# Layer 1's query tokens turned by VectorE with one-piece transfers and kept by squares, and the first batch's gathering in a written order

## The chip, the core and the metric

The kernel runs on one core of one Trainium2 chip. The time is device microseconds of one execution of the whole program; a value for a kernel is the median over several executions. One further execution is recorded by the hardware profiler, and every view quoted below comes from that execution. The engines are named as the profile names them: PE (TensorE matmuls), PEld (TensorE weight loads), DVE (VectorE), ACT (ScalarE), POOL (GpSimd) and SP (SyncE, which issues all DMAs here; its own queue is SPq).

## The reference, cut to what matters

Two batches of 1024 tokens with 256 features pass through two layers. All data are float32.

```python
x = x + L0_xattn(layernorm(x), ctx, ...)      # windowed cross attention, 8 heads
x = x + L0_ffn(layernorm(x), W1, b1, W2, b2)  # 8 groups of 256 tokens, linear
x = x + L1_xattn(layernorm(x), ctx, ...)      # 16 heads of 16, sigmoid scores:
    # q = query @ Wq.T * scale; scores = sigmoid(q k^T); o = (scores v) @ Wo.T
x = x + L1_ffn(layernorm(x), gamma_x, gamma_slot, slot_embeds, w1, w2)
    # xn, se = rms_norm(x), rms_norm(slot_embeds);  logits = xn @ se^T  (1024 slots)
    # slots = softmax_over_tokens(logits)^T @ xn
    # h = gelu(slots @ w1); processed = h @ w2
    # out = softmax_over_slots(logits) @ processed
```

## The kernel before, in words

The tokens are held as four blocks `xq[0..3]` of 512 tokens, each a tile of 128 partitions by 4 subtiles by 256 features; blocks 0 and 1 are batch 0, blocks 2 and 3 are batch 1. A matmul contracts over partitions, so a block that is to be multiplied from its feature side must first be turned: features onto partitions, tokens along the row.

The kernel has two ways to turn a block. `transposed` (line 120) lets PE multiply 128x128 pieces with an identity into a PSUM bank, eight of them for a block (line 125), and copies each of the two banks to SBUF with `nc.any.tensor_copy` (line 126), where the framework picks ACT or DVE. `turned` (line 128) lets DVE transpose 32x32 squares (four instructions at line 134, 128x256 each) into a tile `tr`, and then moves the squares across partitions with 16 DMAs from SP (line 143). In `turned` each DMA moves 32 partitions by 1 KB, but writes it in eight pieces of 128 B, since the destination row runs in token order.

The stages, in the order in which PE passes them: layer 0 (projections, `product`, `bias_rows`, `feed_forward`) up to about 103 us; layer 1's attention, a loop over the four blocks `q` and two halves `c` (`queries` at line 1120, scores at line 1187 with ACT's tanh at line 1196, `poT` at line 1221, `output` at line 1134), up to about 172 us; the logits of both batches (`logits`, line 223) up to 226 us; then for each batch the gathering of slots (`gather`, line 330), `hidden` (line 405), `processed` and `combined` (line 475).

Around the change: `layernorm` (line 704) computes the moments, writes the normalised block `hn` on DVE (line 708) and calls `transposed`. Layer 1's queries use it four times, `hTs[0]` before the loop and `hTs[q + 1]` inside it, on tiles `hn_a` and `hT_a`; layer 0's feed-forward uses it as `norm_ff` on `hn_f` and `hT_f`. The normalised slot rows are turned by `turn_slot_rows` into `seT` (through `tr_se`), and the tokens of the soft mixture by `turn_tokens` into `xhT` (through `tr_m`). `seT` is the moving operand of every logits matmul:

```python
    rhs=seT[:, n, dc, :],       # line 226, 512 elements in one run
    rhs=hTs[q][:, dc, :],       # line 1123, queries
```

The framework orders the instructions of each engine before the run: a planner simulates the program and takes the ready instruction that was emitted first. Each engine then runs its list strictly in that order. Three things bind the planner. `tc.keep_in_program_order` (the argument `late`) pins an instruction behind the one that was emitted just before it on its engine. Inside `tc.manual_schedule(engines=...)` the named engines keep the emission order among the instructions of the region, while where these fall among instructions from outside the region is still the planner's. A nested region orders only the engines that the enclosing one does not. From line 1237 on ACT is ordered this way.

In the last loop, `gather(b, c)` multiplies eight token tiles `lgs[b][s]` (`psl`), DVE writes the scaled slots `sl` (lines 338 and 340), `turn_slots` turns them (`pst`, line 349), and `turn` transposes parts of `ec` on DVE (line 275) and moves them with 16 DMAs from SP (line 284). `largest` and `spread` (lines 295 to 314) build the column maxima `mb` through `dg`; `less` (POOL, line 319) and `dispatch` (ACT, line 322) then prepare each `lgs[b][s]`.

Of the kernel before, what the change touches and what calls it, by code (L numbers as in the profile page):

```python
# [9 lines left out]
FP = mybir.dt.float32  # L10
# [5 lines left out]
P = 128  # L16
# [3 lines left out]
DC = D // P  # L20
NK = 64
QT = 4
QN = QT * P
NQ = B * S // QN
# [18 lines left out]
EC = NSLOT // P  # L43
ST = S // P
XW = D + 2
SQ = 32
R4 = P // SQ


@with_exitstack  # L50
def tile_kernel(
# [51 lines left out]
        ALU.add,  # L103
    )

    seT = const.tile([P, 2, DC, 512], FP, tag="seT", name="seT")

    def moments(xt, name):

# [7 lines left out]
        nc.gpsimd.tensor_tensor(rstd, rstd, m_half, ALU.pow)  # L117
        return mv, rstd

    def transposed(src, dst, name, side=0):  # L120

        for c in range(DC):
            pt = bank(f"pt_{name}_{c}", side)
            for t in range(QT):
                nc.tensor.transpose(pt[:, ts(t, P)], src[:, t, ts(c, P)], ident)  # L125
            nc.any.tensor_copy(dst[:, c, :], pt)

    def turned(src, dst, tr, late=False):

        for t in range(QT):
            turn = nc.vector.transpose(
                tr[:, :, :, t, :].rearrange("p r c n -> p c r n"),
                src[:, t, 0:D].rearrange("p (c r n) -> p c r n", c=DC, r=R4),
            )
            if late:
                tc.keep_in_program_order(turn)
        to = dst.rearrange("p c (t i n) -> p (c t) i n", t=QT, i=R4)  # L140
        for i in range(R4):
            for r in range(R4):
                nc.sync.dma_start(
                    out=to[ts(r, SQ), :, i, :],
                    in_=tr[ts(i, SQ), r].rearrange("p c t n -> p (c t) n"),
                )


    outr = out.rearrange("(q t p) d -> q p t d", t=QT, p=P)
# [61 lines left out]
    def logits(b, s):  # L211

        q, t = b * QB + s // QT, s % QT
        if s == 0:
            zcs[b] = stat.tile([P, ST], FP, tag="zc", name=f"zc_{b}")
            rmaxs[b] = pools["md"].tile([P, NSLOT], FP, tag="rmax", name=f"rmax_{b}")
        lg = keep[b].tile([P, NSLOT], FP, tag=f"lg_{s}", name=f"lg_{b}_{s}")
        lgs[b][s] = lg
        nm = stat.tile([P, 2], FP, tag="nm", name=f"nm_{b}_{s}")
        for n in range(NSLOT // 512):  # L220
            pl = bank(f"pl_{b}_{s}_{n}", 0)
            for dc in range(DC):
                nc.tensor.matmul(  # L223
                    pl,
                    lhsT=xhTs[q][:, dc, ts(t, P)],
                    rhs=seT[:, n, dc, :],
                    start=(dc == 0),
                    stop=(dc == DC - 1),
                )

            nc.vector.tensor_tensor_reduce(  # L231
                lg[:, ts(n, 512)], pl, zero.to_broadcast([P, 512]), -1.0,
                BIG if n == 0 else nm[:, 0:1], ALU.add, ALU.min, nm[:, n : n + 1],
            )

            rm = rmaxs[b][:, ts(n, 512)]
            if s == 1:
                nc.vector.scalar_tensor_tensor(
                    rm, lgs[b][0][:, ts(n, 512)], -1.0, pl, ALU.mult, ALU.max
                )  # L240
            elif s > 1:
                nc.vector.tensor_tensor(rm, rm, pl, ALU.max)
        if t == 0:

            ecs[q] = keep[b].tile([P, 2, QT, 512], FP, tag=f"ec_{q % QB}", name=f"ec_{q}")
        nc.scalar.activation(  # L246
            ecs[q][:, :, t, :],
            lg.rearrange("p (h n) -> p h n", h=2),
            AF.Exp,
            bias=nm[:, 1:2],  # L250
            scale=-1.0,
            accum_out=zcs[b][:, s : s + 1],
        )
# [35 lines left out]
    def largest(b):  # L289

        mT = stat.tile([P, EC], FP, tag="mT", name=f"mT_{b}")
        for h in range(EC // 4):
            pm = bank(f"pm_{b}_{h}", 1)
            for c in range(4):
                nc.tensor.transpose(pm[:, ts(c, P)], rmaxs[b][:, ts(4 * h + c, P)], ident)
            nc.vector.tensor_reduce(
                mT[:, ts(h, 4)], pm.rearrange("p (c n) -> p c n", c=4), AX.X, ALU.max
            )
        dg = pools["mw"].tile([P, EC, P], FP, tag="dg", name=f"dg_{b}")
        nc.vector.tensor_tensor(  # L300
            dg,
            ident.unsqueeze(1).to_broadcast([P, EC, P]),
            mT.unsqueeze(2).to_broadcast([P, EC, P]),
            ALU.mult,
        )
        mTs[b] = dg
# [11 lines left out]
    def less(b, s):  # L318
        nc.gpsimd.tensor_tensor(lgs[b][s], lgs[b][s], mbs[b], ALU.add)  # L319
# [368 lines left out]
    with (  # L688
# [12 lines left out]
        pes = fr[:, NCT : NCT + NPE].rearrange("p (c s) -> p c s", c=DC)  # L701
        b1s = fr[:, NCT + NPE :].rearrange("p (g c) -> p g c", g=NG)

        def layernorm(xt, name, side=0):
            mv, rstd = moments(xt, name)
            hn = lnp.tile([P, QT, D], FP, tag="hn", name=f"hn_{name}")
            for t in range(QT):
                nc.vector.tensor_scalar(  # L708
                    hn[:, t, :], xt[:, t, :], mv[:, t, 0:1], rstd[:, t : t + 1],
                    ALU.subtract, ALU.mult,  # L710
                )
            hT = lnp.tile([P, DC, QN], FP, tag="hT", name=f"hT_{name}")
            transposed(hn, hT, name, side)
            return hT

        wide = ExitStack()
# [62 lines left out]
        def bias(g):  # L779
            pb = bank(f"pbs_{g}", 1)  # L780
            nc.tensor.matmul(pb[:, 0:D], lhsT=ones, rhs=b2z[:, g, :], start=True, stop=True)
            bs = ffc.tile([P, D], FP, name=f"bs_{g}")
            nc.any.tensor_copy(bs, pb[:, 0:D])
            bss.append(bs)
# [2 lines left out]
        hTfs = {}  # L787

        def norm_ff(q, side=0):
            hTfs[q] = layernorm(xq[q], f"f0_{q}", side)  # L790

        def feed_forward(q, side=0):
            for i in range(QN // GN):
# [244 lines left out]
        with (  # L1038
# [21 lines left out]
            def turn_slot_rows(h):  # L1060

                for c in range(h * QT, (h + 1) * QT):
                    tc.keep_in_program_order(
                        nc.vector.scalar_tensor_tensor(
                            se[:, c, :], se[:, c, :], sn[:, c : c + 1], gg, ALU.mult, ALU.mult
                        )
                    )
                tr = lnp.tile([P, R4, DC, QT, SQ], FP, tag="tr", name=f"tr_se_{h}")
                turned(se[:, ts(h, QT), :], seT[:, h], tr, late=True)

# [39 lines left out]

            hTs, qTs, oTs = {}, {}, {}

            def queries(q):
                qTs[q] = a1.tile([P, C1, QN], FP, tag="qT", name=f"qT_{q}")
                for c in range(C1):
                    pq = bank(f"pq_{q}_{c}", 1)
                    for dc in range(DC):
                        nc.tensor.matmul(  # L1120
                            pq,
                            lhsT=wq1s[:, dc, ts(c, P)],
                            rhs=hTs[q][:, dc, :],
                            start=(dc == 0),
                            stop=(dc == DC - 1),
                        )
                    nc.any.tensor_copy(qTs[q][:, c, :], pq)
# [16 lines left out]
                    )  # L1144

            slot_norms()
            hTs[0] = layernorm(xq[0], "a1_0", 1)
            product(7)
            norm_ff(NQ - 1)
            turn_slot_rows(0)  # L1150
            bias_rows(7)


# [17 lines left out]
            )  # L1171
            queries(0)
            bias(7)
            work = ExitStack()
            for q in range(NQ):
                b = q * QN // S
                oTs[q] = a1.tile([P, C1, QN], FP, tag="oT", name=f"oT_{q}")
                for c in range(C1):
                    if c == 1 and q == 0:
                        turn_slot_rows(1)  # L1180
                    if c == 0 and q > 1:
                        norm_tokens(q - 2)
# [16 lines left out]
                    if c == 0:  # L1199
                        if q == 0:  # L1200
# [4 lines left out]
                            pools["mw"] = work.enter_context(  # L1205
                                tc.tile_pool(name="mw", bufs=1, reuse_waits="tile")
                            )
                        if q + 1 < NQ:
                            hTs[q + 1] = layernorm(xq[q + 1], f"a1_{q + 1}", 1)
                        if q > 0:  # L1210
                            output(q - 1, (0, 1) if q + 1 < NQ else (0,))
                        if 0 < q < 3:
# [21 lines left out]

    ctx.enter_context(tc.manual_schedule(engines={mybir.EngineType.Activation}))
    open_keep(1)
    open_pool("slp", side="right")
    for u in range(1, B * ST + 2):  # L1240
# [29 lines left out]
    nc.sync.dma_start(out=ms, in_=m12_in)  # L1270
    for b in range(B):
        slTs[b] = pools["slp"].tile([P, DC, NSLOT], FP, tag="slT", name=f"slT_{b}")
        for c in range(EC):
            gather(b, c)
            if c > 0:
                turn_slots(b, c - 1)
            if b == 0 and c in (1, 3, 5):
                turn(c // 4, c // 2 % 2, c == 5)
            if b == 1 and c % 2 == 0:
                turn(QB + c // 4, c // 2 % 2, True)  # L1280
            if b == 0:
                less(1, c)
                if c > 0:
                    dispatch(1, c - 1)
        if b == 0:
            dispatch(1, ST - 1)
            sum_weights()
        hidden(b)
        with tc.manual_schedule(engines={mybir.EngineType.DVE, mybir.EngineType.PE}):
            processed(b)  # L1290
            combined(b)

# [69 lines left out]
```

## Time and profile before

| what | value |
|---|---|
| median of 3 runs | 444.54 us (443.05 to 444.97) |
| the profiled execution's own time | 443.19 us |
| its span, first to last instruction | 441.4 us |
| PE busy | 430.4 us, 97% of the span |
| PEld busy | 319.1 us, 72% |
| DVE busy | 328.4 us, 74% |
| ACT busy | 114.7 us, 26% |
| POOL busy | 84.7 us, 19% |
| mean granted TensorE clock | 0.999 |

Busy time is a sum over an engine's instructions. The span leaves out 1.8 us of the profiled execution's own time. A matmul of float32 operands appears as two records, so `x16` stands for eight matmuls. The line numbers are those of the kernel before.

### The profile page before, as it was taken

What the parts mean: (1) busy time and instruction counts of PE and PEld (TensorE: products, weight loads), DVE (VectorE), ACT (ScalarE), POOL (GpSimd) and SP (SyncE); (2) the same over time, 40 slices, a digit from 0 to 9 for tenths busy, and PEclk for the clock granted to TensorE, in tenths of its full rate; (3) what the DMA queues carried; (4) which work ended last, traced back from release to release, by engine and by line L of the source; (5) the groups of instructions that cost most, each with busy time, mean ns of one, the idle gap of its engine ahead of it and who ended that gap; (6) DMA issues with size and microseconds to landing.
All of it is one profiled execution on the core that took longest, in us unless ns stands there. A gap on an engine that the chain in (4) does not pass through costs nothing.

```text
span 441.4 us, 6412 instructions
## 1 busy us (share of the span) xinstructions
PE 430.4 (97%) x2368; PEld 319.1 (72%) x2368; DVE 328.4 (74%) x735; ACT 114.7 (26%) x213; POOL 84.7 (19%) x84
## 2 busy tenths in 40 slices
PE   6999999999999999999999999999999999999996
PEld 5788898888645545444458864699998884499996
DVE  0587989899284787998787259995995568796956
ACT  1212334112345441343573405510000002530000
POOL 3012232234212111200887930000000000000000
PEclk9999999999999999999999999999999999999999
DMA  8996595400202132321043633332003666600002
GB/s 269 415 422 274 224 379 206 170 0 7 42 10 39 21 47 30 48 32 18 0 162 72 98 52 50 45 56 43 1 0 103 97 90 99 90 1 1 1 1 97
DMA packets 100641, 42.08 MB, mean 95 GB/s; under 512 B 94593, under 2 KB 96769, under 8 KB 99201
## 3 DMA queue, kind: packets, MB, share of 16 engines
q1 hardware_dynamic: 100610, 41.67, 35.4%
q8 instruction: 19, 0.31, 0.3%
q14 instruction: 12, 0.10, 0.1%
HBM read 28.03 MB, written 2.10 MB: 68 GB/s over the span
## 4 chain that ended last, share of the span: by engine, by line
PE 81%; DVE 15%; POOL 1%; ACT 1%; issue 1%; DMA 1%; ACTq 0%; POOLq 0%
PE psl L330 12%; PE pl L223 12%; PE pp L475 11%; PE pc L475 11%; PE pmh L405 11%; PE pmt L744 5%; DVE b2z L775 5%; PE pq L1120 3%; PE pf L1134 3%; PE psg L1187 2%; PE poT L1221 2%; PE po L802 2%; DVE hn_f L708 1%; DVE bn_f L113 1%; DVE bn_a L113 1%; PE pt_a L125 1%
## 5 line engine op out<-in xcount | busy, mean ns | idle before, releaser
L744 PE MATMUL pmt<-wg 128*128 128x256 f32 x256 | 58.9, 388 | 3.8 <-DMA wg<-in_wff_dram 3.8
L330 PE MATMUL psl<-xh,lg 128*128 128x258 f32 x256 | 58.7, 381 | 0.0
L744 PEld LDWEIGHTS pmt<-wg 128*128 128x128 f32 x256 | 49.2, 195 | 10.7 <-DMA wg<-in_wff_dram 4.1
L223 PE MATMUL pl<-seT,xhT 128*128 128x512 f32 x128 | 55.9, 593 | 0.0
L330 PEld LDWEIGHTS psl<-xh,lg 128*128 128x128 f32 x256 | 47.3, 190 | 7.1 <-issue 0.5
L223 PEld LDWEIGHTS pl<-seT,xhT 128*128 128x128 f32 x128 | 24.2, 190 | 29.1 <-issue 24.9
L319 POOL TENSOR_TENSOR lg<-lg,mb 128x1024 f32<-128x1024 f32 x16 | 37.2, 2361 | 30.8 <-DVE mb L172 30.8
L475 PEld LDWEIGHTS pp<-ms,mh 128*128 128x128 f32 x256 | 29.4, 192 | 1.0 <-issue 1.0
L475 PE MATMUL pp<-ms,mh 128*128 128x128 f32 x256 | 29.7, 276 | 0.0
L246 ACT ACTIVATE ec<-lg,nm 128x1024 f32<-128x1024 f32 x16 | 18.4, 1148 | 40.4 <-DVE nm L231 40.4
L775 DVE SCALAR_TENSOR_TENSOR b2z<-wg,fr,b2z 128x256 f32<-128x256 f32 x48 | 24.6, 516 | 0.5
L415 ACT ACTIVATE mh<-mh 128x512 f32<-128x512 f32 x32 | 19.2, 627 | 20.3 <-DVE mh L448 17.7
L405 PE MATMUL pmh<-slT,ms 128*128 128x512 f32 x48 | 24.0, 592 | 0.0
L475 PE MATMUL pc<-pr,ec 128*128 128x128 f32 x192 | 22.1, 275 | 0.0
L475 PE MATMUL pp<-m_sums,mh 128*128 128x128 f32 x192 | 22.1, 275 | 0.0
L338 DVE RECIPROCAL rz<-psl 128x1 f32<-128x1 f32 x16 | 2.5, 156 | 26.0 <-PE psl L330 26.0
L475 PEld LDWEIGHTS pc<-pr,ec 128*128 128x128 f32 x192 | 21.8, 192 | 0.0
L475 PEld LDWEIGHTS pp<-m_sums,mh 128*128 128x128 f32 x192 | 21.8, 192 | 0.0
L1196 ACT ACTIVATE sg<-psg 128x512 f32<-128x512 f32 x32 | 16.5, 603 | 17.0 <-PE psg L1187 17.0
L275 DVE STREAM_TRANSPOSE tr<-ec 128x512 f32<-128x512 f32 x32 | 20.1, 679 | 0.0
L322 ACT ACTIVATE lg<-lg 128x1024 f32<-128x1024 f32 x16 | 16.5, 1049 | 12.4 <-POOL lg L319 12.4
L486 DVE TENSOR_TENSOR mh<-mh,mh 128x1024 f32<-128x1024 f32 x16 | 18.5, 1219 | 1.5 <-PE pp L475 1.5
(187 smaller groups left out, 703.9 us busy)
## 6 DMA issues: line engine op xcount, KB each, us to landing
wg<-in_wff_dram SPq DMA_DIRECT2D x6, 2048.0 KB, 14.3
ec<-tr SPq DMA_DIRECT2D x128, 64.0 KB, 2.3
xT<-in_xT_dram SPq DMA_DIRECT2D x4, 512.0 KB, 12.8
x<-in_x_dram SPq DMA_DIRECT2D x4, 512.0 KB, 15.0
wg<-in_wff_dram SPq DMA_DIRECT2D x2, 1024.0 KB, 10.6
xhT<-tr_m SPq DMA_DIRECT2D x64, 32.0 KB, 2.0
ms<-in_m_dram SPq DMA_DIRECT2D x1, 2048.0 KB, 7.9
out_dram<-x SPq DMA_DIRECT2D x16, 128.0 KB, 1.8
```

Of the source, the lines that this page charges most:

```text
L223: nc.tensor.matmul(pl, lhsT=xhTs[q][:, dc, ts(t, P)], rhs=seT[:, n, dc, :], start=(dc == 0), stop=(dc == DC - 1),)
L246: nc.scalar.activation(ecs[q][:, :, t, :], lg.rearrange("p (h n) -> p h n", h=2), AF.Exp, bias=nm[:, 1:2], scale=-1.0, accum_out=zcs[b][:, ...
L275: ins = nc.vector.transpose(tr[:, :, :, t, :].rearrange("p r c n -> p c r n"), half[:, t, :].rearrange("p (c r n) -> p c r n", c=EC // 2, ...
L319: nc.gpsimd.tensor_tensor(lgs[b][s], lgs[b][s], mbs[b], ALU.add)
L322: nc.scalar.activation(lgs[b][s], lgs[b][s], AF.Exp, scale=-1.0)
L330: nc.tensor.matmul(pz[:, 0:XW], lhsT=lgs[b][s][:, ts(c, P)], rhs=xhs[b * QB + s // QT][:, s % QT, :], start=(s == 0), stop=(s == ST - 1),)
L405: nc.tensor.matmul(to, lhsT=lefts[i][:, ts(j, P)], rhs=slTs[b][:, i, 0:512] if i < 2 else rights[b][i], start=True, stop=True,)
L415: nc.scalar.activation(h, h, AF.Gelu)
L475: nc.tensor.matmul(to, lhsT=left(k, m), rhs=right[:, k, :], start=(k == 0), stop=(k == QT - 1),)
L486: nc.vector.tensor_tensor(dst, x, y, op)
L744: nc.tensor.matmul(pm[:, ts(hc, D)], lhsT=w1g[:, oc, ts(hc, P)], rhs=w2g[:, oc, :], start=(oc == 0 and hc == 0), stop=(oc == OC - 1 and hc ...
L775: nc.vector.scalar_tensor_tensor(acc, weights[g][1][:, oc, :], b1s[:, g, oc : oc + 1], acc, ALU.mult, ALU.add)
```

## The change

1. Layer 1's query blocks no longer pass through PE. `norm_queries(q)` normalises the block as before (`normed`) and calls `turned_by_square`: DVE's four transposes into `tr_a`, then 16 DMAs into `hTs[q]`, whose layout is now by squares, so that each DMA writes 1 KB per partition in one piece. Three `hTs` buffers are kept. Blocks 0, 1 and 2 are emitted before the loop, block 3 in its first round.
2. `seT` is laid out in the same way and filled with `turned_by_square`.
3. The two matmul groups that read them take the tokens through `in_order`, a view of 16 runs of 32 elements.
4. `turn_slot_rows(0)` is emitted later, after `bias(7)`, and `turn_slot_rows(1)` one round later.
5. `norm_ff` copies PSUM to SBUF on ACT for blocks 2 and 3; before, the framework chose.
6. The first batch's gathering loop is a region in which DVE and PE keep the emission order. Its three `turn` calls come after steps 0, 1 and 4 instead of 1, 3 and 5, and the last of them is no longer pinned.
7. `dg` moves from its own buffer to the buffer of `mb` (batch 0) or `rmax` (batch 1).

```diff
+IN_ORDER = {mybir.EngineType.DVE, mybir.EngineType.PE}
+ACT_ORDER = {mybir.EngineType.Activation}
...
-    seT = const.tile([P, 2, DC, 512], FP, tag="seT", name="seT")
+    seT = const.tile([P, 2, R4, DC, QT, SQ], FP, tag="seT", name="seT")
...
-    def transposed(src, dst, name, side=0):
+    def transposed(src, dst, name, side=0, out=nc.any.tensor_copy):
...
-            nc.any.tensor_copy(dst[:, c, :], pt)
+            out(dst[:, c, :], pt)
...
+    def turned_by_square(src, dst, tr, late=False):
+
+        squares(src, tr, late)          # the four DVE transposes, as in turned()
+        for i in range(R4):
+            for r in range(R4):
+                nc.sync.dma_start(
+                    out=dst[ts(r, SQ), i].rearrange("p c t n -> p (c t n)"),
+                    in_=tr[ts(i, SQ), r].rearrange("p c t n -> p (c t n)"),
+                )
+
+    def in_order(x, dc):
+
+        return x[:, :, dc].rearrange("p i t n -> p t i n")
...
-                    rhs=seT[:, n, dc, :],
+                    rhs=in_order(seT[:, n], dc),
...
-        dg = pools["mw"].tile([P, EC, P], FP, tag="dg", name=f"dg_{b}")
+        dg = pools["md"].tile([P, EC, P], FP, tag=("mb", "rmax")[b], name=f"dg_{b}")
...
         def norm_ff(q, side=0):
-            hTfs[q] = layernorm(xq[q], f"f0_{q}", side)
+            out = nc.any.tensor_copy if q < QB else nc.scalar.copy
+            hTfs[q] = layernorm(xq[q], f"f0_{q}", side, out)
...
-                turned(se[:, ts(h, QT), :], seT[:, h], tr, late=True)
+                turned_by_square(se[:, ts(h, QT), :], seT[:, h], tr, late=True)
...
+            def norm_queries(q, late=False):
+
+                hn = normed(xq[q], f"a1_{q}")
+                hTs[q] = a1.tile([P, R4, DC, QT, SQ], FP, tag="hTa", name=f"hTa_{q}", bufs=3)
+                tr = lnp.tile([P, R4, DC, QT, SQ], FP, tag="tr", name=f"tr_a_{q}")
+                turned_by_square(hn, hTs[q], tr, late)
...
-                            rhs=hTs[q][:, dc, :],
+                            rhs=in_order(hTs[q], dc),
...
             slot_norms()
-            hTs[0] = layernorm(xq[0], "a1_0", 1)
+            norm_queries(0)
             product(7)
             norm_ff(NQ - 1)
-            turn_slot_rows(0)
+            norm_queries(1)
+            norm_queries(2)
             bias_rows(7)
...
             queries(0)
             bias(7)
+            turn_slot_rows(0)
             work = ExitStack()
             for q in range(NQ):
...
                 for c in range(C1):
                     if c == 1 and q == 0:
+                        norm_queries(3, True)
+                    if c == 1 and q == 1:
                         turn_slot_rows(1)
...
-                        if q + 1 < NQ:
-                            hTs[q + 1] = layernorm(xq[q + 1], f"a1_{q + 1}", 1)
...
-        for c in range(EC):
-            gather(b, c)
-            if c > 0:
-                turn_slots(b, c - 1)
-            if b == 0 and c in (1, 3, 5):
-                turn(c // 4, c // 2 % 2, c == 5)
+        with tc.manual_schedule(engines=(IN_ORDER, ACT_ORDER)[b]):
+            for c in range(EC):
+                gather(b, c)
+                if c > 0:
+                    turn_slots(b, c - 1)
+                if b == 0 and c in (0, 1, 4):
+                    turn(c // 4, c % 2)
...
```

More of the change, by code (lines that the diff above doesn't have):

```diff
@@ L125, in transposed, with squares @@
                 nc.tensor.transpose(pt[:, ts(t, P)], src[:, t, ts(c, P)], ident)
-            nc.any.tensor_copy(dst[:, c, :], pt)
-    def turned(src, dst, tr, late=False):
+            out(dst[:, c, :], pt)
+    def squares(src, tr, late=False):
         for t in range(QT):
@@ L139, in turned @@
                 tc.keep_in_program_order(turn)
+    def turned(src, dst, tr):
+        squares(src, tr)
         to = dst.rearrange("p c (t i n) -> p (c t) i n", t=QT, i=R4)
@@ L702, in tile_kernel, with normed @@
         b1s = fr[:, NCT + NPE :].rearrange("p (g c) -> p g c", g=NG)
-        def layernorm(xt, name, side=0):
+        def normed(xt, name):
             mv, rstd = moments(xt, name)
@@ L711, in layernorm @@
                 )
+            return hn
+        def layernorm(xt, name, side=0, out=nc.any.tensor_copy):
+            hn = normed(xt, name)
             hT = lnp.tile([P, DC, QN], FP, tag="hT", name=f"hT_{name}")
-            transposed(hn, hT, name, side)
+            transposed(hn, hT, name, side, out)
             return hT
@@ L1231, in tile_kernel @@
             output(NQ - 1)
-    ctx.enter_context(tc.manual_schedule(engines={mybir.EngineType.Activation}))
+    ctx.enter_context(tc.manual_schedule(engines=ACT_ORDER))
     open_keep(1)
@@ L1272, in tile_kernel @@
         slTs[b] = pools["slp"].tile([P, DC, NSLOT], FP, tag="slT", name=f"slT_{b}")
-        for c in range(EC):
-            gather(b, c)
-            if c > 0:
-                turn_slots(b, c - 1)
-            if b == 0 and c in (1, 3, 5):
-                turn(c // 4, c // 2 % 2, c == 5)
[L1279 to L1282, printed above, removed]
-                if c > 0:
-                    dispatch(1, c - 1)
+        with tc.manual_schedule(engines=(IN_ORDER, ACT_ORDER)[b]):
+            for c in range(EC):
+                gather(b, c)
+                if c > 0:
+                    turn_slots(b, c - 1)
+                if b == 0 and c in (0, 1, 4):
+                    turn(c // 4, c % 2)
+                if b == 1 and c % 2 == 0:
+                    turn(QB + c // 4, c // 2 % 2, True)
+                if b == 0:
+                    less(1, c)
+                    if c > 0:
+                        dispatch(1, c - 1)
         if b == 0:
@@ L1288, in tile_kernel @@
         hidden(b)
-        with tc.manual_schedule(engines={mybir.EngineType.DVE, mybir.EngineType.PE}):
+        with tc.manual_schedule(engines=IN_ORDER):
             processed(b)
```

## The prediction

> **What bounds the kernel now.** I read first the table by stretches of the span, then who waited on PE, then the chain that ended last in order of time, and last the DMA issues and DVE's and SP's own instructions around the change.
>
> The table by stretches has for each engine its busy time and record count; the first figure after the stretch is its length.
>
> ```profile
> 99.00:165.00 66.00, 65.65 (x335) 39.42 (x336) 45.29 (x125) 26.94 (x54) 13.18 (x18) 1.00 0.18 27
> 165.00:226.00 61.00, 60.93 (x163) 28.05 (x162) 50.70 (x134) 22.88 (x35) 19.14 (x15) 1.00 0.16 24
> 226.00:233.00 7.00, 6.33 (x28) 4.21 (x27) 4.94 (x7) 5.62 (x7) 4.00 (x2) 1.00 0.83 303
> 233.00:259.00 26.00, 26.00 (x128) 22.48 (x127) 12.09 (x30) 8.46 (x8) 23.63 (x12) 1.00 0.52 78
> ```
>
> The reader is to see PE without a hole in all four (65.65 of 66.00 us, 26.00 of 26.00) at a granted clock of 1.00, and DVE with room in the first (45.29 of 66.00). A microsecond of PE work taken out here ends the program a microsecond earlier, as long as nothing new makes PE wait. The waits on PE, in whole:
>
> ```profile
> PE pmt L744 <- DMA wg<-in_wff_dram: 3.8, 1, 3.8
> ...
> PE pb L314 <- DVE dg L300: 0.7, 1, 0.7
> ...
> PE po L802 <- DVE hT_f L126: 0.4, 1, 0.4
> ```
>
> The 3.8 us stands at the start of the program. The 0.4 us is one that the change touches: a feed-forward of layer 0 waits for the second half of a turned block, copied by DVE. The chain in order of time (start, length) shows the four turnings that are to go:
>
> ```profile
> 105.69 0.87 PE pt_a L125 x8
> ...
> 123.83 0.87 PE pt_a L125 x8
> ...
> 131.40 1.07 PE psg L1187 x8
> 132.47 1.02 PE pt_a L125 x8
> 133.49 3.46 PE pf L1134 x16
> ...
> 144.71 1.02 PE pt_a L125 x8
> ...
> 155.88 1.07 PE psg L1187 x8
> 156.95 1.93 PE pf L1134 x8
> ```
>
> All four lie on the chain, between PE work on both sides.
>
> **What goes: 3.5 us of PE.** Four blocks of eight transposes, one record each. Where PE changes from `psg` to another form some 0.15 us is added to whatever follows: `pt_a` takes 1.02 after `psg` and 0.87 elsewhere, and `pf` x8 takes 1.93 after `psg` where half of 3.46 is 1.73. That addition passes to `pf`, so I count 4 x 0.87 = 3.48. PE starts a transpose every 0.109 us (0.87/8), while its record lasts 273 ns; the records overlap. The Trainium skill (TensorE: Matmul & The Clock Gate, Part 4: PE-mode transpose) gives about 275 ns for one in a kernel and says that the full clock does not engage for it. By that figure 32 of them would be an estimated 8.8 us; the trace has the record's length alike, but starts 0.109 us apart at clock 1.00, so the row decides.
>
> The eight PSUM copies into `hT_a` go too (five on ACT at 0.59 us, three on DVE at 0.67 us). Nobody but `pq` waited for them.
>
> **Feed-forward copies on ACT: 0.4 us.** `pt_f` of block 2 ends at 97.85 us; ACT copied the first half from 97.62 to 98.21, DVE the second from 98.62 to 99.30, and PE stood 0.40 us. With both on ACT the second ends about 98.80, just as PE has finished what it has (its last record before the wait starts at about 98.5 and ends at 98.95). Gain 0.4, at worst 0.
>
> **What comes on DVE: hidden.** Per block four transposes, 128x256, at 0.335 us a start (four in 1.42 us for `tr_se`): 5.7 us in all, less 2.0 of copies. Block 0 falls before 99 us, where DVE is busy 36.3 of 39.0 us, but it is ahead: the bias sums of group 7 end at 96.4 us and PE uses them at 118.5. The other three fall between 102 and 131 us, where the slot rows' 1.4 us at 106 move away. If the cover fails, one block's 1.4 us would show.
>
> **What comes on SP, and whether the blocks land in time.** 64 DMAs are added to SP's one queue, and 32 (`seT`) change shape. No row has 32 partitions by one piece of 1 KB. From above: the eight-piece transfers, 609 ns each on SP and 2.0 us to land. From below: the loads of one piece per partition, 328 ns. The output stores, 128 partitions by one 1 KB piece, are the nearest in shape: 337 at least, 400 in the median. I take 0.40, so a block is 6.4 us of SP and lands 2 us later.
>
> ```profile
> 107.66 32.28 SPq L143 DMA_DIRECT2D seT<-tr_se  x32
> 148.53 52.76 SPq L143 DMA_DIRECT2D xhT<-tr_m  x64
> ```
>
> SP is idle before 107.66 since its last weight load at 75.7 us, which is no longer queued behind anything of this change if block 0 is normalised where it is now (83.3 to 84.6 us). I follow each block. Block 0: transposes by 86, landed by 95; queries at 115. Block 1: its input is final at 97.0, normalising at about 102.5, transposes by 105, landed by 114; queries at 126.7 less 1.7 saved by then, so 125.0. Block 2: input at 106.2, its `hn` buffer free after `pt_f` at 113.5, transposes by 116, landed 125; needed at about 136. Slot rows 0: behind `vsum` (115.2), transposes by 119, landed 131. Block 3: input at about 123.7, transposes at 130, landed 139; needed at 148. Slot rows 1: behind `oT` of block 1 (about 136), landed 148; needed by the first logits. `xhT` of block 0, still in eight pieces: transposes at 148.4 less 3.2, so 145.2; 16 x 0.61 and 2.0 bring it to 157.0. The first logits matmul (162.97 before) wants it at 159.5. All in time, with 2.5 us left where 2.6 were before. A `tr` buffer is reused every second block; each earlier user has landed by then.
>
> Two new waits on DVE have something behind them: slot rows 1 and block 3 sit between `oT` instructions that `pf` wants at once, with no `pt_a` in between to cover. The pair at 155.88 and 156.95 shows `pf` following `psg` directly without a hole, `oT` being done meanwhile. I take 0 and keep 1 us as the upper end.
>
> **Strided reads by PE: 0.** 80 matmuls (160 records of 0.43 us, 68 us together) read 16 runs of 32 elements. The nearest row is `pk` at line 1077, whose moving operand is two runs of 64: 0.89 us for eight records, 111 ns each, against 112 ns for contiguous 128-column products (25.10 us for 224, line 475). One break costs nothing that 0.01 us in eight records can show; at that grain (1.3 ns) 15 breaks in 160 records could be 3 us. Below nothing is excluded, since a contiguous read is already at PE's pace. I take 0, keep 3.
>
> **The written order: 0.4 us lost.** At 226 to 233 us PE fills the wait for `dg` with 16 records of `psl`.
>
> ```profile
> 226.16 1.47 PE L330 MATMUL psl<-xh,lg 128*128 128x258 f32 x6
> 227.47 0.60 PE L295 MATMUL pm<-ident,rmax 128*128 128x128 f32 x4
> 227.90 2.56 PE L330 MATMUL psl<-xh,lg 128*128 128x258 f32 x10
> 231.14 1.98 PE L314 MATMUL pb<-dg,ones 128*128 128x512 f32 x4 [0.67 <-DVE dg L300]
> ```
>
> ACT prepares `lgs[0][4..7]` only from 227.80 to 231.68, 0.97 us each, so these 16 cannot be step 0 alone; some belong to step 1. In emission order step 1 must follow step 0's last: 14 records fit before `pb`, and two (2 x 0.22) come later. The region leaves `pb`'s place to the planner, so the fill itself stays; were it lost whole, it costs 16 x 0.22 = 3.5. Behind 233 us PE is full either way, and the order of `psl` and `pst` is the same. `turn` after step 4 waits about 1 us on DVE for its buffer's DMAs (issued 236 to 247, landed 249); `sl` of step 5 is queued behind it and is ready at 253, needed at 255. `dg` in other buffers: `mb`'s copies must wait for all of `pb`, which DVE's copy, the last one, did anyway: 0.
>
> **Sum.** -3.5 - 0.4 + 0.4 = -3.5 us. The profiled execution took 443.2 us (span 441.4 and 1.8 around it): 439.7. It lies at the low end of the three runs (443.05 to 444.97); their middle is 444.0, so I add 0.8 and forecast 440.5 as a median, 0.9% under 444.54.
>
> A rule speaks against the change: the Trainium skill (VectorE: DVE Perf Modes, Rules for kernel authors) would turn 128x128 on TensorE where PSUM will do. By path length the rows agree with it: 0.87 and two copies of 0.6 are 2.1 us, the new way 1.4 + 6.4 + 2.0 = 9.8. Were that on the path, four blocks would cost 4 x 7.7 = 31 us more; by the times above none is.
>
> **Rivals.** *SP's queue becomes the bound (slower).* If one-piece transfers take SP as long as the eight-piece ones, the queue never empties from block 2 on: 116 + 64 x 0.61 + 9.8 + 2.0 = 166.8 us for the first `xhT`, wanted at 159.5. PE stands 7.3 us there: 439.7 + 7.3 + 0.8 = 447.8. It decides from 0.50 us an issue on (116 + 64x + 11.8 = 159.5). For it: 609 ns in 96 such rows; against: 328 to 400 in every one-piece row. *The gain is eaten (no change).* The planner orders anew from simulated landing times; a fill of the kind at 226 us lost whole (3.5) or an `oT` or a block late by 2 to 3 us leaves 442.5 to 444.5. For it: PE's strict order and 64 more DMAs it must guess; against: the margins above, mostly over 8 us. *Strided reads cost (slower).* From 5% on the 68 us they eat the whole gain; at 10%, 447.3. Against: `pk`.
>
> **Chances.** Forecast 0.64 (its own range 438.5 to 442.0), SP's queue 0.12, gain eaten 0.18, strided reads 0.06. The range for 8 in 10 runs from 438.5 to 445.0: it takes in the forecast and the eaten gain and leaves out the two slower ones. About 0.5% (2.2 us) can be told from no change here: faster 0.66 (the forecast and the best of the eaten gains), within 0.5% 0.17, slower 0.17.
>
> **What would show it.** Right: no `pt_a` in the chain, `pq` and `pl` still at 0.43 us a start, DMAs into `hTa` and `seT` at about 0.4 us on SP, PE's stretch from 99 us to the first logits 3.9 us shorter, `pb` about 3.5 us earlier. Wrong: a wait of `pq` or `pl` on `tr_a`, `tr_se` or `tr_m`; `pf` waiting for `oT`; a longer hole at `dg`; a later last weight load on SP.

## The result, and the profile after

The changed kernel took 455.63 us in the median of six executions (455.17 to 457.22), the kernel before 444.36 in the median of six (443.05 to 444.97) on the same chip: a ratio of 1.026, with a 95% interval of 1.024 to 1.028. The forecast was 440.5 us. The profiled execution took 455.48 us, with a span of 453.7 us.

The table by stretches, for the first two of the four shown of before (length; then busy us and records of PE, PEld, DVE, ACT and POOL; granted clock; DMA share; GB/s):

```profile
99.00:165.00 66.00, 61.85 (x298) 35.58 (x296) 47.35 (x134) 24.70 (x50) 14.25 (x18) 0.97 0.20 45
165.00:226.00 61.00, 52.87 (x137) 24.78 (x138) 41.80 (x115) 15.20 (x24) 7.05 (x10) 0.92 0.22 33
```

Before, PE stood 0.35 us in the first and 0.07 in the second; now it stands 4.15 and 8.13, and the granted clock, 1.00 before, is 0.97 and 0.92. (The other two stretches now hold other work, since all from 180 us on runs 12 us later.) The waits on PE say whom it stood for:

```profile
PE pl L243 <- DMA xhT<-tr_m: 9.5, 1, 9.5
...
PE pf L1166 <- DVE oT L1262: 2.7, 1, 2.7
...
PE psl L350 <- ACT lg L342: 0.6, 2, 0.4
PE pb L334 <- DVE dg L320: 0.6, 1, 0.6
```

Two of these are new and large: 9.5 us before the first logits, for a transfer, and 2.7 us before a `pf`, for DVE. The 0.4 us for `hT_f` is gone. SP's own instructions show where both come from (start, length; 48 issues in one line are three blocks):

```profile
90.13 39.66 SPq L159 DMA_DIRECT2D hTa<-tr_a  x48
129.90 10.03 SPq L159 DMA_DIRECT2D seT<-tr_se  x16
140.04 10.02 SPq L159 DMA_DIRECT2D hTa<-tr_a  x16
150.16 10.90 SPq L159 DMA_DIRECT2D seT<-tr_se  x16
161.18 53.18 SPq L149 DMA_DIRECT2D xhT<-tr_m  x64
```

Sixteen one-piece transfers take SP 10.0 us, 0.63 from start to start; the median record is 589 ns, where the eight-piece ones have 609. From 108.1 to 171.7 us, where the first block's `xhT` is out, SP has no pause over 0.44 us. The first `xhT`, whose squares DVE had finished by 149.7, is issued at 161.18 and landed at 173.0. The chain that ended last shows both holes:

```profile
127.93 3.10 DMA hTa<-tr_a
...
131.16 1.42 DVE tr_a L133 x4
132.58 0.65 DVE oT L1262
133.27 4.96 PE pf L1166 x14
...
171.04 1.95 DMA xhT<-tr_m
...
173.13 5.91 PE pl L243 x8
```

In the first four lines DVE cannot turn block 3, since its `tr` buffer still holds block 2, whose last transfer lands at 131.0; `oT` stands behind that on DVE, and PE behind `oT`. In the last two the transfer ends PE's long wait. Besides, `pf` x14 takes 4.96 us (3.29 at the full clock) and `pl` x8 5.91 (3.60 before): the granted clock was 0.73 from 134 to 139 us and 0.67 from 173 to 180.

Just ahead of the first `xhT` the chain lists a `tr_m` at 159.82 us. By DVE's own records that is block 1's; block 0's had been there since 149.7. The chain names the releaser that came last by the records; what the issue waited for was its turn in the queue.

The place where PE fills the wait for `dg`, now (the timeline of PE, from the second `psl` group on):

```profile
240.03 0.60 PE L350 MATMUL psl<-xh,lg 128*128 128x258 f32 x2
241.02 0.70 PE L350 MATMUL psl<-xh,lg 128*128 128x258 f32 x2 [0.39 <-ACT lg L342]
241.97 0.70 PE L350 MATMUL psl<-xh,lg 128*128 128x258 f32 x2 [0.24 <-ACT lg L342]
243.24 1.98 PE L334 MATMUL pb<-dg,ones 128*128 128x512 f32 x4 [0.57 <-DVE dg L320]
```

In the written order PE waits for `lg` twice and puts 12 records ahead of `pb` where 16 were (the prediction had counted on 14). From the last group but one of `pm` to the first `pst` it is 11.61 us (237.82 to 249.43), 10.76 before.

### The profile page after: what moved, and what is told of

It is laid out like the page before. It is cut to its first block, busy times and chain, and to the rows that moved or that the text cites. A ratio compares the mean times of both kernels' runs of the same rounds, so it can differ in the third digit from the quotient of the medians.

```text
span 453.7 us, 6450 instructions
## 1 busy us (share of the span) xinstructions
PE 430.9 (95%) x2336; PEld 317.6 (70%) x2336; DVE 330.6 (73%) x746; ACT 113.0 (25%) x210; POOL 85.3 (19%) x84
## 4 chain that ended last, share of the span: by engine, by line
PE 72%; DVE 16%; SPq 6%; DMA 2%; issue 2%; ACT 1%; POOL 1%; ACTq 0%; DVEq 0%; POOLq 0%
PE pl L243 13%; PE psl L350 12%; PE pp L495 11%; PE pc L495 11%; PE pmh L425 11%; DVE b2z L799 4%; SPq L159 4%; PE pmt L768 3%; PE pf L1166 3%; SPq L149 2%; DVE hn_f L728 2%; PE pq L1152 2%; PE poT L1255 1%; DVE bn_f L115 1%; DVE bn_a L115 1%
## 5 line engine op out<-in xcount | busy, mean ns | idle before, releaser
L243 PE MATMUL pl<-seT,xhT 128*128 128x512 f32 x128 | 58.2, 613 | 9.5 <-DMA xhT<-tr_m 9.5
L768 PEld LDWEIGHTS pmt<-wg 128*128 128x128 f32 x256 | 49.2, 194 | 10.7 <-DMA wg<-in_wff_dram 3.9
L251 DVE CUSTOM_DVE_ANT_0 lg<-pl,zero 128x512 f32<-128x512 f32 x16 | 10.9, 678 | 14.4 <-PE pl L243 14.4
L1166 PE MATMUL pf<-w1s,oT 128*128 128x256 f32 x64 | 17.3, 420 | 2.7 <-DVE oT L1262 2.7
```

Source lines behind the costliest of these rows:

```text
L243: nc.tensor.matmul(pl, lhsT=xhTs[q][:, dc, ts(t, P)], rhs=in_order(seT[:, n], dc), start=(dc == 0), stop=(dc == DC - 1),)
L768: nc.tensor.matmul(pm[:, ts(hc, D)], lhsT=w1g[:, oc, ts(hc, P)], rhs=w2g[:, oc, :], start=(oc == 0 and hc == 0), stop=(oc == OC - 1 and hc ...
L1166: nc.tensor.matmul(pf[:, ts(k, D)], lhsT=oTs[q][:, c, ts(2 * i + k, P)], rhs=wo1s[:, c, :], start=(c == 0), stop=(c == C1 - 1),)
```

## The experiments

Four theories. **S:** SP needs some 0.63 us for an issue whatever its pieces, and 96 issues ahead of the first `xhT` make it late. **B:** the two `tr` buffers make DVE wait, and `oT` behind it. **R:** PE is slowed by reading 16 runs of 32. **W:** the written order costs 0.85 us. "Before" is the kernel before, run on the same chip in the same series: 443.3 us in the first two series, 443.6 and 444.2 in the others.

**four_issues: the same bytes in a quarter of the issues.**

```diff
-        for i in range(R4):
-            for r in range(R4):
-                nc.sync.dma_start(out=dst[ts(r, SQ), i]..., in_=tr[ts(i, SQ), r]...)
+        for i in range(R4):
+            nc.sync.dma_start(out=dst[ts(i, SQ)]..., in_=tr[ts(i, SQ)]...)
```

> Each block and each half of the slot rows moves in 4 DMAs of 32 partitions x 4 KB in place of 16 of 32 partitions x 1 KB: the same bytes, a quarter of the issues (the squares stay in their group of partitions, so the values read differ; PE's work is the same). Theory S (SP's queue: about 0.63 us an issue whatever its pieces, 96 of them ahead of the first xhT): 72 issues fewer take 45 us off the queue, xhT is issued as soon as tr_m is turned (about 146) and lands near 157, both holes (9.5 and 2.7 us) and the low clock behind them go: 439 to 442. Theory R (PE is slowed by what it reads, 16 runs of 32): nothing changes in PE's reads, so 455. If an issue's time goes with its bytes (4 KB: 4 times as long), SP is as full as before: 455. Theory W (the written order alone) 455.

Measured: 439.78 us, 0.992 of before (0.990 to 0.994). SP's instructions:

```profile
139.47 2.42 SPq L158 DMA_DIRECT2D seT<-tr_se  x4
145.79 52.50 SPq L149 DMA_DIRECT2D xhT<-tr_m  x64
```

This kernel leaves out the crossing of partitions, so its output is another one. An issue of 4 KB a partition holds SP as long as one of 1 KB did (0.59 us in the median), the first `xhT` goes out at 145.79, as the forecast had it (145.2), and neither hole is left; the clock is 1.00 from 8.5 us to the end of PE's work. Everything else of the change is still in it, the strided reads and the written order among them. So S holds, R falls, and W is small. The longest row of `pl` says the same of R, before and in the changed kernel:

```profile
210.21 15.61 PE L223 MATMUL pl<-seT,xhT 128*128 128x512 f32 x36
222.33 15.61 PE L243 MATMUL pl<-seT,xhT 128*128 128x512 f32 x36
```

The time is close to the forecast's (440.5), but with SP held 2.4 us for a block, and not the 6.4 that the forecast had.

**tr_three: a third `tr` buffer.**

```diff
-  tag="tr"                    # tr_se, tr_a
+  tag="tr", bufs=3
...
-  tag="xhT", bufs=3
+  tag="xhT", bufs=2           # for the space
```

> The changed kernel with three tr buffers in place of two (one xhT buffer less, for the space). Theory B (DVE stands on a tr buffer, oT is queued behind it): the two DVE waits of 3.3 us go, and the hole of 2.7 us before pf at 133 with them and the low clock behind it (1.9): 455.6 - 4.6 = 451. Theory S (the sum of the issues on SP): the hole at 133 goes too, but xhT of block 0 still lands at 173, since SP's queue is full from 108 on, so PE stands longer before pl (9.5 + 4.6 = 14 us): 455 to 456.

Measured: 455.44 us, 1.027 (1.025 to 1.030). Waits on PE:

```profile
PE pl L243 <- DMA xhT<-tr_m: 8.7, 1, 8.7
...
PE pq L1152 <- DMA hTa<-tr_a: 3.6, 1, 3.6
```

DVE's waits on `tr` and the hole before `pf` are gone, and the time stays. SP issues the first `xhT` at 161.75 (161.18 in the changed kernel). The hole did not all go to `pl`, as I had said: 3.6 us stand before `pq`, because block 3's transfers now come too late for a PE that is 3.9 us ahead (`psg` at 146.72 for 150.57). B is a symptom of S here.

**pe_queries: the query blocks back on PE, all else as changed.**

```diff
-            norm_queries(0)
+            hTs[0] = layernorm(xq[0], "a1_0", 1)      # and so for blocks 1 to 3, as before
...
-                            rhs=in_order(hTs[q], dc),
+                            rhs=hTs[q][:, dc, :],
```

> The changed kernel with the query blocks turned on PE as before (64 issues fewer on SP, 32 transposes back on PE); the slot rows stay in squares and are read so, the feed-forward copies stay on ACT, the gathering stays in its written order. S: the loss goes with the queue: 444.4 - 0.4 (copies on ACT) + 0.85 (written order) = 444.8. R: pl still reads seT in runs of 32, 96 of its 160 strided records remain: 447 or more. If the loss were the written order's: 454.

Measured: 448.51 us, 1.011 (1.008 to 1.014): none of the three. The hole is still there, smaller (2.7 us for `xhT` and a `pl` x8 of 5.37 us). SP's instructions tell why:

```profile
118.88 33.94 SPq L159 DMA_DIRECT2D seT<-tr_se  x32
152.94 53.30 SPq L149 DMA_DIRECT2D xhT<-tr_m  x64
```

Before, the 32 issues for `seT` began at 107.66 and the first `xhT` at 148.53; here they begin at 118.88, because the change emits the slot rows later, and `xhT` goes out 4.4 us later with no query transfer in the queue at all (its squares were ready at 149.06, 0.6 us later than before; the rest is the queue). My expectation had counted what the queue holds and not where the slot rows stand in it. Hole 2.7, clock 1.8, written order 0.9 and 0.4 gained make 5.0; 5.2 were measured.

**two_blocks: the kernel before with blocks 0 and 1 by VectorE.**

```diff
+            NDVE = 2
...
-                        if q + 1 < NQ:
+                        if NDVE <= q + 1 < NQ:
                             hTs[q + 1] = layernorm(xq[q + 1], f"a1_{q + 1}", 1)
```

> The kernel before with blocks 0 and 1 of the queries turned by VectorE and one-piece transfers and read in squares; blocks 2 and 3 on PE, slot rows in eight-piece transfers and the gathering as before; feed-forward copies of the later blocks on ACT. 32 issues are added to SP, of which the last lands before 116, so that the slot rows and xhT go out as before. S: xhT lands in time, 444.4 - 2 x 0.87 - 0.4 = 442.2. R: 32 strided pq of 64: some 446.

Measured: 440.38 us, 0.993 (0.991 to 0.995), faster than both kernels. The slot rows fill SP from 118.1 to 140.7 us, and the first `xhT` goes out as soon as it is turned:

```profile
90.05 27.96 SPq L138 DMA_DIRECT2D hTa<-tr_a  x32
118.11 22.60 SPq L158 DMA_DIRECT2D seT<-tr_se  x32
145.89 53.83 SPq L158 DMA_DIRECT2D xhT<-tr_m  x64
```

**three_blocks, and three_blocks_tr3: one block more, and a third `tr` buffer with it.** (The edit is `NDVE = 3`; then `bufs=3` for `tr` and `bufs=2` for `xhT`.)

> As two_blocks, with block 2 too turned by VectorE: 16 issues more on SP. S, from the times of two_blocks (slot rows done on SP at 140.7, xhT started at 145.9, landed near 158, wanted at 159.5 and now 0.9 earlier): 16 issues of 0.63 put xhT's start at 150.8 and its landing at 162.9, so a hole of 4.3 us less 0.87 saved: 440.4 + 3.4 = 443.8, and up to 1.8 more where the clock falls behind the hole. Were the queue's place free, as the 0.40 of the forecast has it: 439.5.

> three_blocks, which took 454.6, with a third tr buffer (one xhT buffer less). In three_blocks DVE stood 10.0 us on a tr buffer whose transfers were late in SP's queue, oT behind it, PE 10.7 us behind oT. If the buffers bound it there, both go and what is left is the queue's length: 48 issues of 0.63 from 118.5 on put block 2's landing at 137 (wanted at 135.4) and the start of xhT at 148.7, landing at 160.8: holes of 1.6 and some 0.6 us, 440.4 - 0.9 + 2.2 = 441.7. If the queue alone bound it, with or without the buffer, the hole moves to pq or pl and the time stays at 454.

Measured: 454.57 us, 1.024 (1.023 to 1.026), and with the third buffer 443.83, 1.000 (0.998 to 1.001). The 16 issues of block 2 cost 14 us, where I had said 3.4. The waits, on PE and then on DVE:

```profile
PE pf L1168 <- DVE oT L1264: 10.7, 1, 10.7
...
DVE tr_se L149 <- DMA hTa<-tr_a: 13.4, 2, 10.0
```

Here it is B: the planner put block 2 behind six issues of the slot rows, the buffer that DVE wanted came free at 138.5 us, and the second half of the slot rows, `oT` and PE stood for it in a row. (The first of DVE's two waits, 3.4 us, delays `vsum`, and PE stands 2.5 us before a `po` for that.) `pl` then waits for nothing, for PE is later than `xhT`. With a third buffer, and block 2 behind ten issues of the slot rows, the 10.7 us become 0.6, and what is left is the queue's length: 1.4 us before `pl` (for the 0.6 expected) and 0.5 before `pq`. The executions of that kernel spread from 442.4 to 445.5 us, and the profiled one is the fastest of them; what spreads them, I have not settled. So the queue is one cause, and where it shows depends on who needs the late transfer first: the consumer, or DVE for the buffer.

**queue_scalar and queue_gpsimd: the 64 query transfers issued by ACT or by POOL.**

```diff
-                turned_by_square(hn, hTs[q], tr, late)
+                turned_by_square(hn, hTs[q], tr, late, nc.scalar)   # or nc.gpsimd
```

> The changed kernel with the 64 transfers into hTa issued by ACT in place of SP; order of PE's work as in the changed kernel. S: SP has only the slot rows before xhT; the second half goes out at about 139.5 to 150 as it does where the blocks need four issues each, xhT behind it lands at 162, wanted at 159.4: a hole of 2.7 us and a low clock for 1.8 in place of 14.4 and 4: 444 plus what 64 issues of 0.6 us put in front of ACT's own copies (0 to 6 us). R or W: 455.

> As the other, but issued by POOL, which has less to do that PE waits for (rstd of each block). S: 444 plus 0 to 3 us for rstd standing behind issues. If what costs is the transfers themselves (their time on the DMA engines, not their issue), either queue leaves the holes: 455.

Measured: 461.56 us, 1.040 (1.037 to 1.043), and 452.75 us, 1.022 (1.017 to 1.027). The hole before `pl` shrinks as S has it (2.9 and 3.2 us for 9.5), but the price moves with the issues. On ACT, a burst of them stands ahead of the copies and the tanh that PE waits for:

```profile
PE poT L1255 <- ACT sg L1232: 9.0, 2, 6.1
```

On POOL an issue takes 0.50 us, and the holes are 2.8 us for `vsum` and 1.8 for `oT`, both on DVE, which had itself waited 8.5 us for POOL's `rstd_a` behind the issues, plus a `po` at half the clock behind the first (6.68 us for 3.72). Its executions spread from 451.1 to 455.5 us. Neither extra price was in my expectation in that size.

**shapes: four shapes of the same block.**

```diff
+        # block 0: 16 x (32 partitions, 1 KB)   block 1: 4 x (32 partitions, 4 KB)
+        # block 2:  4 x (128 partitions, 1 KB)  block 3: 1 x (128 partitions, 4 KB)
```

> The changed kernel with the query blocks moved in four shapes: block 0 as in the changed kernel (16 DMAs of 32 partitions x 1 KB), block 1 in 4 of 32 x 4 KB, block 2 in 4 of 128 x 1 KB, block 3 in 1 of 128 x 4 KB; in blocks 1 to 3 the squares stay in their group of partitions, so other values are read. What one issue holds SP is read from its records. If it is a price of the issue: about 0.6 us in all four. If it goes with the partitions: 0.6, 0.6, 2.4, 2.4. If a record of 128 partitions x 1 KB costs what the output stores of that shape do: 0.34 to 0.40 for block 2. Time with 25 issues in place of 64: 440.

Measured: 441.51 us in one execution. SP's instructions, one line for each shape:

```profile
89.96 10.12 SPq L179 DMA_DIRECT2D hTa<-tr_a  x16
107.89 2.42 SPq L159 DMA_DIRECT2D hTa<-tr_a  x4
114.37 2.46 SPq L166 DMA_DIRECT2D hTa<-tr_a  x4
...
128.75 0.51 SPq L172 DMA_DIRECT2D hTa<-tr_a  x1
```

The medians are 589, 592, 599 and 511 ns, for 32 KB, 128 KB, 128 KB and 512 KB. It is a price of the issue, whatever the bytes and the partitions; the one issue of block 3 follows a pause, and the first behind a pause took 507 ns in block 1 too. The third line settles my nearest row: 128 partitions by one piece of 1 KB is the shape of the output stores, which took 337 ns at least and 400 in the median; inside SBUF it takes 599. (Blocks 1 to 3 leave out the crossing of partitions here, so the output is another one.)

**no_written and written_only: the written order taken out of the changed kernel, and put alone into the kernel before.** (The edit is the last hunk of the change, undone in the one and done in the other, with `dg` in its new buffers in both.)

> The changed kernel without the written order of the first batch's gathering (the planner orders it as before). W: the distance from the last pm to the first pst falls by 0.85 us and the three small holes at psl go: 454.8. If the planner orders the layer ahead of it otherwise too, up to 2 us either way. S: the holes at pf and at pl stay.

> The kernel before with the first batch's gathering in its written order and dg in the other buffers, nothing else. W (three small holes at psl and a shorter fill, 0.85 us, read from the changed kernel): 443.3 + 0.85 = 444.2. Against W, the changed kernel without the order was not faster (456.15 and 455.63), because a hole of 1.9 us at pmh came in its place: where the planner's own order loses as much elsewhere, 443.3.

Measured: 456.15 us, 1.029 (1.027 to 1.032), and 444.31 us, 1.0013 (1.0001 to 1.0025). Without it, the changed kernel loses nothing at `pb` (9.90 us from `pm` to `pst`, for 11.61), but gets a hole of 1.9 us before `pmh` and behind it a clock of 0.50 from 275.73 to 279.14, so that nothing is gained. Alone it adds 0.7 us by the medians, just clear of the noise, and from `pm` to `pst` 0.86 (11.62 for 10.76). W holds against the order that the kernel before had, and not against the one that the planner finds in the changed kernel.

**mixed: all four blocks by VectorE, blocks 2 and 3 issued by POOL, the slot rows early.**

```diff
-                    if c == 1 and q == 0:
+                    if c == 0 and q == 1:
                         turn_slot_rows(1)
+                        norm_queries(3, True)       # its 16 transfers, and block 2's, from nc.gpsimd
```

> All four query blocks turned by VectorE and read in squares, the slot rows in eight-piece transfers on SP where the kernel before has them (block 3 and the second half right behind oT of block 0), blocks 0 and 1 issued by SP, blocks 2 and 3 by POOL (0.50 us an issue); gathering as before. S: no hole at pl if the second half of the slot rows is on SP by 136 and block 3 lands by 146: 440.4 - 2 x 0.87 = 438.6. If POOL's rstd stand behind its issues as where POOL had all four: some 3 us more, 441 to 442.

Measured: 446.53 us, 1.005 (1.004 to 1.007; 444.3 to 447.7, the profiled execution the fastest). POOL issues block 3 from 137.2 to 145.2 us, `rstd_m` of the tokens stands behind it, DVE waits 2.7 us for that, the first `xhT` goes out at 151.3 and not 145.9, and PE stands 1.8 us before `pl`; 2.5 us more for `vsum`, and 1.6 before `pmh`. POOL's queue is no free place either.

## Why the prediction was wrong

The step that failed is a term of the sum: "I take 0.40, so a block is 6.4 us of SP". A block is 10.0 us. The bounds beside it were 0.328 and 0.609; the value was taken from the output stores because they were "the nearest in shape", and the shape plays no part (the run of four shapes). The row that was nearest in its two ends, SBUF to SBUF, was the eight-piece one, and it was right to within 4%. The landing times went with it: block 2 at 131.0 us and not 125, slot rows 0 at about 141 and not 131, block 3 at 151 and not 139, and `xhT` at 173.0 and not 157.0. Two readings beside it were off by less. DVE turned blocks 0 and 1 by 90.0 and 108.0 us, and not by 86 and 105, with `b2z` and other work in between, so that block 1's issues, with which SP's unbroken row begins, started 3 us later. And the 2.6 us that `xhT` was said to have in hand before were 1.7: its 16 issues took 11.4 us there, with one of 1.17 among them, and not 16 x 0.61, and the last landed at 161.3.

| term | forecast | measured |
|---|---|---|
| four blocks off PE, copies on ACT, to the first `pl` without holes | -3.9 us | -3.5 (159.43 for 162.97 in four_issues) |
| strided reads | 0 (up to 3) | 0: `pq` and `pl` 592 ns in the median, 36 records of `pl` in 15.61 us in both kernels |
| `xhT` late | 0 (2.5 in hand) | 9.5 |
| DVE's waits on `tr` | 0 (up to 1) | 2.7 |
| clock behind the two holes | not in the sum | 1.7 + 2.3 = 4.0 |
| written order | +0.4 | +0.9 |
| sum | -3.5 | +13.6 |

On PE the last group of `pc` starts 12.98 us later (446.86 for 433.88), 0.6 us less than the terms add up to; where these went was not followed. The profiled span grew by 12.3, since the last stores held SP 3.91 us and not 4.63, and the medians by 11.3, as the profiled execution of the kernel before lay 1.2 us under its own median.

*What was right.* The gain on PE came, up to the first hole: `psg` at 128.77 for 131.33 us, 2.6 us earlier where two blocks and the 0.4 make 2.1. The 0.4 us for `hT_f` went. Strided reads cost nothing that 160 records show. DVE's own work stayed hidden: in four_issues no wait for it is new.

*The rival that came true* was SP's queue, and its place (PE before the first `pl`) and its kind were right; its threshold (0.50 us an issue) was passed by the 0.63 measured, and no run tried a value near it on SP. It had 0.12. Its price, 447.8, was 8 us short. It let `xhT` land at 166.8: it started block 2 at 116 us, where block 1, itself 10 us long, held SP to 118.1, and it counted the record (0.61) and not the distance from start to start, with two issues of 1.5 and 1.9 us among them (64 issues took 43.0 us, 0.67 each). That is 6.2 us. It had the new waits on DVE at 0, although the same late queue fills the `tr` buffers ("each earlier user has landed by then" rests on the 0.40 too), and it had the clock at 1.00 behind a long hole.

*The rule weighed against the change* (Trainium skill, VectorE: DVE Perf Modes, Rules for kernel authors: 128x128 on TensorE where PSUM will do) bites for four blocks and not for two. By the trace a block's way by DVE is 1.4 + 10.0 + 1.9 = 13.3 us, not 9.8; for blocks 0 and 1 that lies beside other work and the kernel gains 2.9 us, for blocks 2 and 3 it stands in front of the logits.

*What the forecast did not ask* is what the edit does to the order in the queue. The slot rows, emitted later, make `xhT` 4.4 us late even with no query transfer on SP (pe_queries). The prediction followed each transfer by its own due time; the due time of what comes last was the one that counted.

A page of the Trainium skill (DMA: Bandwidth & Descriptors, Issuing engines are not separate DMA queues) says that issuing from several engines saves only the time to initiate a transfer, and that this is "usually small relative to the DMA itself". In this trace it is not small: 0.59 us beside 1.9 us to landing, and 96 at 0.63 are 60 us. The runs on ACT and POOL took this time off SP and put it in front of other work.

## What to carry to other kernels

Count the issues of a queue, not the bytes: many small transfers inside SBUF cost their number times the distance between two starts, and here the row with the same two ends had that distance right where the row of the same shape had not. Then lay out the whole queue in order and ask when the last thing in it starts, for every edit that adds to the queue or moves a place in it. A late queue shows twice, at the consumer and at whoever needs the source buffer again, so taking the second wait away alone (tr_three) gains nothing while the first is there, and the part of a change that fits the queue's idle time (two_blocks) can be kept.

## What the runs showed of the hardware

A DMA inside SBUF held SP for about 0.59 to 0.61 us in a row, with 32 or 128 partitions, one piece or eight, 32 KB or 128 KB, and for 0.51 in most one-piece cases that followed a pause, the one of 512 KB among them. Single issues of 1.0 to 2.0 us stand between these, for a reason not found. Of those with an end in DRAM in the kernel before, the 13 loads of `wg` took 0.33 in the median and the 16 output stores 0.40, but its other single loads 0.31 to 0.75. No run changed the end alone, so that this is what sets them apart is argued and not shown. Issued by POOL the same transfers took 0.50 us.

The granted clock fell to one half behind holes of PE: 0.50 in tr_three from 173 to 177 us, in three_blocks from 144 to 147, in queue_gpsimd from 122 to 127. From 99 us to the end of PE's work no hole up to 1.83 us did this in any run, and every one of 3.63 us and more did. Between them it went both ways: lowered after 1.94 (before `pmh` in no_written), 2.25, 2.67, 2.73, 2.77 and 2.93 us, at 1.00 after 2.31, 2.43, 2.48, 2.54, 2.94 and 3.20. The traces say which. In every run that shows changes of the clock, all of them lie on one grid with a step of 3.41 us (in the changed kernel at 133.28, 136.69, 167.41 and 177.65 us). The clock fell at the end of a step in which PE had stood 1.97 us or more, and stayed at 1.00 where it had stood 1.81 or less; in between lies one step each way, 1.94 lowered (no_written) and 1.95 not (mixed). So a longer hole that falls across two steps can cost nothing. In queue_gpsimd the hole of 2.77 us has 1.97 in one step, and that of 3.20 is shared out as 1.44 and 1.76 (step and its length; busy us and records of PE, PEld, DVE, ACT and POOL; granted clock; DMA share; GB/s):

```profile
118.03:121.44 3.41, 1.44 (x10) 0.31 (x8) 2.02 (x7) 2.51 (x5) 1.35 (x2) 1.00 0.00 0
121.44:124.85 3.41, 2.61 (x6) 2.16 (x7) 3.41 (x12) 0.11 (x1) 2.24 (x5) 0.50 0.12 29
...
165.82:169.23 3.41, 1.97 (x12) 1.42 (x8) 3.13 (x10) 2.06 (x4) 0.00 (x0) 1.00 0.34 50
169.23:172.64 3.41, 1.65 (x4) 0.87 (x5) 0.29 (x3) 0.00 (x0) 2.21 (x3) 1.00 0.32 48
172.64:176.05 3.41, 3.41 (x15) 1.16 (x14) 2.56 (x11) 0.50 (x1) 0.00 (x0) 1.00 0.33 48
```

This is read from the runs at hand; none moved a hole against the grid. Behind a hole that lowered the clock the work took 1.6 to 3.0 us longer, so that such a hole of 2.7 us costs half as much again at least. The Trainium skill (TensorE: Matmul & The Clock Gate, Why this matters for your kernels) warns of idle gaps over about 3 us; half the clock agrees with that page, but 1.94 us was enough in one run and 3.20 was not in another, and a forecast with a hole of 7 us in it should have had this loss in its price.
